# A decoder layer on one core: the fused stage's source rewritten with links a step apart and parts in three places of a step

## The chip, the cores and the metric

The kernel runs on one core of a Trainium2 chip. A core has five engines, each with its own queue of instructions that it works through in order: TensorE (PE, matrix products), VectorE (DVE), ScalarE (ACT), GpSimd (POOL) and SyncE (SP, which here only issues DMAs). Queues meet in semaphores: an instruction that waits holds up all that is behind it in its queue. The metric is the device time of one execution in microseconds (us).

## What is computed

The reference is one decoder layer on `x` of 8 x 512 tokens of 512 features, all in 32-bit floats. Cut to what matters:

```python
x = layernorm(x + mamba(x))          # layernorm, in-projection, convolution over 4 tokens, silu,
                                     # h[t] = exp(A*dt[t]) * h[t-1] + dt[t]*B[t]*x[t]  (1024 channels x 16 states),
                                     # y[t] = sum over states of h[t]*C[t]; y*silu(z), out-projection
x = layernorm(x + attention(x, ctx)) # 16 heads of 32, 512 queries against 512 keys of ctx
x = layernorm(x + moe(x))            # 32 experts, the best 4 of the best 4 groups, 640 places each, and one shared expert
```

Each line needs the one before it, but for one batch row only; the experts need all rows.

## The kernel before

Three stages follow one another: `layers` (mamba, attention, gate and shared expert), `experts`, and `finish` (the last layernorm). The change touches only `layers`, the fused stage, and the helper `layernorm`.

**Chunks and steps.** `layers` runs over 16 chunks: 8 batch rows, each in two halves `t` of 256 tokens. A chunk has 32 steps `k`. A step treats 128 channels and four of the 16 states: four quarters `q` of two channel groups each, four state groups `g`, and the two channel groups in turn. In each step `carry` (L452) allocates one of four buffers `h` and copies the state in, on ACT; `decays` (L446) computes the four exponentials of the *next* step; `scan` forms the input (L458) and runs the recurrence (L462) on DVE; `collect` multiplies by C (L479, DVE) and sums over states with eight matmuls (L483, PE) into the PSUM tile `py`. When a quarter's eight steps are done, `gated` (L495) multiplies the gate `zs` by `py`. The matmuls of a step are the last to read its `h`, so the step four later can only begin when they are done.

**Front work of the mamba part.** Between `scan` and `collect` of certain steps the source calls other functions: `back` of the previous chunk (out-projection, L512, steps 1 and 2), then its residual and layernorm `norm` (L521); `gate_x` (steps 3 to 6), which projects the gate; the silu of `zs` (step 7); `prepare` at steps 3, 11, 19 and 27, which computes `dt` and `dtx` of the next quarter (matmul L398, exponentials L408 to L414 on ACT, `both` L418 to L421 on DVE, and eight DMAs L427 that spread them over partitions); and, for the next chunk, `load_x` (5), `norm_x` (9), `flip_x` (11), `convolve` (12, 15, 18, 21), silu (23) and `x_proj` (24). PSUM for all of these, and for the dense products below, is the tag `mm`, with two buffers.

**Side work.** `sources` and `units` return lists of parts of the attention, the gate and the shared expert of the *previous* batch row: keys and values, queries, the score maxima (`maximum`: L775 on PE, then L777 on DVE), the weights (`weigh`: L801, L805), their sums (`gather`: L817), `divide`, `output`, the gate (`pick`, `choose`, `place`, `locate`), the scatter of tokens to the experts (`send`: L650, indirect DMAs of POOL) and the shared expert (`hidden`, `shared`). Every part has a weight. A running sum of weights, set against `work(k)`, the weight of the mamba part of each step, says how many of them are called in a step, so that the sum grows evenly over two chunks.

**Links.** A part may return a function, its continuation: what DVE or ACT does once PE's product is there. `do` calls a part, then `settle` calls every continuation in `left` once; a continuation may return another, called at the following `settle`. `dry` calls until none is left, and is called where a part is marked `first`.

**Order of the queues.** Before and after, the framework's scheduler decides the order of each engine's queue. It takes the source's order as a preference, but passes over an instruction whose inputs or buffers it takes to be not ready. Only the silu calls and the table load behind them (L362, L363) are tied to the ACT instruction traced before.

Of the kernel before, what the change touches and what calls it, by code (L numbers as in the profile page):

```python
# [17 lines left out]
P = 128  # L18
# [9 lines left out]
T = 256  # L28
# [23 lines left out]
def rsqrt(nc, pool, var, n, name):  # L52

    v = pool.tile([P, n], F32, tag=f"{name}v")
    nc.vector.tensor_scalar(v, var, EPS, None, ALU.add)
    r = pool.tile([P, n], F32, tag=f"{name}r")
    nc.scalar.activation(r, v, AF.Ln)
    nc.scalar.activation(r, r, AF.Exp, scale=-0.5)
    m = pool.tile([P, n], F32, tag=f"{name}m")
    nc.vector.tensor_tensor(m, v, r, ALU.mult)  # L60
    nc.vector.tensor_tensor(m, m, r, ALU.mult)
    nc.vector.tensor_scalar(m, m, -0.5, 1.5, ALU.mult, ALU.add)
    o = pool.tile([P, n], F32, tag=f"{name}o")
    nc.vector.tensor_tensor(o, r, m, ALU.mult)
    return o


def layernorm(nc, pool, tiles, outs, name):

    n = len(tiles)  # L70
    mv = pool.tile([P, n, 2], F32, tag=f"{name}mv")
    for j, t in enumerate(tiles):
        st = pool.tile([P, 6], F32, tag=f"{name}st")
        nc.vector.bn_stats(st, t)
        nc.vector.bn_aggr(mv[:, j, :], st)
    r = rsqrt(nc, pool, mv[:, :, 1], n, name)
    less = pool.tile([P, n], F32, tag=f"{name}less")
    nc.vector.scalar_tensor_tensor(less, mv[:, :, 0], -1.0, r, ALU.mult, ALU.mult)
    for j, (t, o) in enumerate(zip(tiles, outs)):
        nc.scalar.activation(o, t, AF.Identity, bias=less[:, j : j + 1], scale=r[:, j : j + 1])  # L80


def layers(ctx, tc, a, x1d, filld, based, xbuf):
# [193 lines left out]

    def load_x(b, t, f):
        f["xt"] = xt = mp.tile([P, NT_, D], F32, tag="xt", name="xt")
        nc.sync.dma_start(xt, a["x"][b, t * T : (t + 1) * T, :].rearrange("(j p) d -> p j d", p=P))  # L280

    def norm_x(f):
        xt = f["xt"]
        xs = [xt[:, j, :] for j in range(NT_)]
        layernorm(nc, sm, xs, xs, "ln1")
# [34 lines left out]
    def convolve(t, q, f):  # L320
# [4 lines left out]
        def first_tap():  # L325
# [23 lines left out]
            return other_taps  # L349
# [43 lines left out]
    def prepare(q, f):  # L393
# [8 lines left out]
        def exponentials():  # L402
# [13 lines left out]
            def both():  # L416
# [12 lines left out]
                return lambda: timesD  # L429
# [8 lines left out]
            return both  # L438
# [16 lines left out]
    def scan(t, c, g, dtx, bc, da, h):  # L455
# [4 lines left out]
        )  # L460
        flat = h.rearrange("p n t -> p (n t)")
# [4 lines left out]
    def collect(c, g, h, bc, py, f):  # L466


        if g == 0:
            for j in range(2):  # L470
                nc.tensor.matmul(
                    py[j * HP : (j + 1) * HP, c % 2, :],
                    ident[:, j * HP : (j + 1) * HP],
                    f["xs"][c // 2][:, c % 2, :],
                    start=(c % 2 == 0),
                    stop=False,
                )
        steps = h.rearrange("p (j m) t -> p j m t", j=2)[:, :, :, 1:]
        nc.vector.tensor_tensor(steps, steps, bc[1], ALU.mult)  # L479
        for m in range(NG // 2):  # L480
            for j in range(2):
                s = (g, m, c % 2)
                nc.tensor.matmul(  # L483
                    py[j * HP : (j + 1) * HP, c % 2, :],
                    twice,
                    h[:, j * 2 + m, 1:],
                    start=False,
                    stop=(s == (NST // NG - 1, NG // 2 - 1, 1)),
                )

    def gated(q, f, py):

        f["xs"].pop(q)
        pair = f["zs"][:, 2 * q : 2 * q + 2, :]
        nc.vector.tensor_tensor(pair, pair, py, ALU.mult)  # L495
# [6 lines left out]
    def back(half, b, t, f):  # L502
# [15 lines left out]
        def norm():  # L518
# [3 lines left out]
            layernorm(nc, sm, outs, outs, "ln2")  # L522
            r0 = b * S + t * T
            nc.sync.dma_start(x1d[r0 : r0 + T, :].rearrange("(j p) d -> p j d", p=P), o)

        return norm
# [15 lines left out]
    def pick(b, x2t, x2T, st):  # L542
# [8 lines left out]
        return lambda: choose(b, x2t, pl, st)  # L551

    def choose(b, x2t, pl, st):
# [34 lines left out]
        for k in range(K):  # L588
            nc.vector.tensor_reduce(w[:, :, k : k + 1], work, AX.X, ALU.max)
            oh = gm.tile([P, SC, E], F32, tag=f"g_oh{k}", name="g_oh")  # L590
            nc.vector.tensor_tensor(
                oh, work, wide(w[:, :, k : k + 1], [E]), ALU.is_equal
            )
# [3 lines left out]
            nc.vector.tensor_tensor(oh, early, wide(m2, [E]), ALU.is_equal)  # L597
            if k < K - 1:
                nc.vector.scalar_tensor_tensor(work, oh, -4.0, work, ALU.mult, ALU.add)
            picked.append(oh)  # L600
        ws = new([1], "g_ws")
        nc.vector.tensor_reduce(ws, w, AX.X, ALU.add)
        nc.vector.tensor_scalar(ws, ws, 1e-9, None, ALU.add)
        nc.vector.reciprocal(ws, ws)

        any_ = new([E], "g_any")
        nc.vector.tensor_tensor(any_, picked[0], picked[1], ALU.add)
        nc.vector.tensor_tensor(any_, any_, picked[2], ALU.add)
        nc.vector.tensor_tensor(any_, any_, picked[3], ALU.add)
        nc.vector.tensor_tensor(sc, sc, any_, ALU.mult)  # L610
        nc.vector.tensor_tensor(x2t[:, :, D : D + E], sc, wide(ws, [E]), ALU.mult)
        nc.gpsimd.iota(
            x2t.bitcast(I32)[:, :, D + E :], pattern=[[P, SC], [0, 1]], base=b * S, channel_multiplier=1
        )
        st["picked"] = picked, any_

    def place(picked, any_, st):
# [7 lines left out]
        return lambda: locate(picked, pb, pn, st)  # L625

    def locate(picked, pb, pn, st):
# [16 lines left out]
        nc.vector.tensor_scalar(dest, ds_, float(SLOTS), None, ALU.add)  # L644

# [69 lines left out]
    def units(b):  # L715
# [20 lines left out]
        def flip(j):  # L736
            xr = st.pop(("xr", j))
            if j + 1 < SC:
                fetch(j + 1)
# [102 lines left out]
        def divide(oc):  # L842

            attT, total = st["attT"], st["total"]
            r = p3.tile([P, D], F32, tag="row", name="r")
            nc.scalar.activation(r, total, AF.Ln)
            nc.scalar.activation(r, r, AF.Exp, scale=-1.0)
            nc.vector.tensor_tensor(total, total, r, ALU.mult)
            nc.vector.scalar_tensor_tensor(total, total, -2.0, r, ALU.add, ALU.mult)
            nc.vector.scalar_tensor_tensor(  # L850
                attT[:, oc, :], attT[:, oc, :], -1.0, total, ALU.mult, ALU.mult
            )

        def output(lt):
# [9 lines left out]
            def add_up():  # L864
                nc.vector.tensor_tensor(xr, pp, xr, ALU.add)
                nc.vector.tensor_tensor(st["x2"][lt], xr, bo, ALU.add)
                if lt == SC - 1:
                    layernorm(nc, sm, st["x2"], st["x2"], "ln3")
# [12 lines left out]
        def hidden(name, ic):  # L881
# [8 lines left out]
            def use():  # L890
                if name == "sw3":
                    nc.vector.tensor_tensor(hT[:, ic, :], hT[:, ic, :], ps, ALU.mult)  # L892
                    return
                nc.scalar.copy(hT[:, ic, :], ps)
                if ic == DC - 1:
                    silu(hT)
# [20 lines left out]
        todo += more[:-2]  # L917
        add(0, begin)
        add(0, fetch, 0)
        todo += more[-2:]  # L920
        for j in range(SC):
            add(0.5, flip, j)
# [32 lines left out]
        for lt in range(SC):  # L955
            add(3.4, output, lt)
# [11 lines left out]
        for ic in range(DC):  # L968
            add(3.4, hidden, "sw3", ic)
            if ic == (0 if end else 3):  # L970
                add(0.5, lambda: place(*st["picked"], st))
# [3 lines left out]
        for j in range(SC):  # L975
            add(3.4, shared, j, dry=(j == 0))
            if b < B - 1:
                add(*sends[j])
# [24 lines left out]
    left = []  # L1003

    def settle():

        got = [part() for part in left]
        left[:] = [x for x in got if x]

    def dry():  # L1010
        while left:
            settle()

    def do(fn, *args, first=False):

        if first:
            dry()
        rest = fn(*args)
        settle()
        if rest:  # L1020
            left.append(rest)

    def work(k):

        front = 6.9 if k in (1, 2) else 3.4 if 3 <= k < 7 or k in (12, 15, 18, 21, 24) else 1.0 if k in (11, 26) else 0.0
# [3 lines left out]
    norm_x(f)  # L1029
# [14 lines left out]
    decays(0, 0, f["ready", 0][0], das[0])  # L1044
    old, side, cleared = None, [], 0

    for i, (b, t) in enumerate(chunks):
# [7 lines left out]
        py = None  # L1055
        for k, (q, g, ci) in enumerate(steps):
# [5 lines left out]
            h = carry(t, 2 * q + ci, g)  # L1062
# [417 lines left out]
```

## Time and profile before

| | us |
|---|---|
| Median of three runs (5550.69 to 5557.85) | 5556.39 |
| The profiled execution | 5555.79 |
| Its span, from the first to the last instruction | 5554.1 |
| PE busy | 4883.9 (88%) |
| DVE busy | 4349.2 (78%) |
| ACT busy | 2592.8 (47%) |
| POOL busy | 560.9 (10%) |
| First scan to end of the last scan (the fused stage) | 3630.0 |
| From there to the end | 1867.5 |

In the profile, L12 is line 12 of the kernel before. Lines of instructions give start, duration, engine, line, operation, output and inputs with their shapes, a count where several were merged, and in brackets the idle time of the engine just before, with what ended it. Waits are given as who waited, for whom, the total, how often and the longest. Matmuls overlap one another, so PE's busy time says only that it had work. An engine's idle time matters only where that engine is the late one.

### The profile page before, as it was taken

The numbers are of one execution on the slowest core, as the hardware profiler recorded it, in microseconds if no ns is written. First come the engines' busy times: TensorE is split into PE (matmuls) and PEld (weight loads), VectorE is DVE, ScalarE is ACT, GpSimd is POOL, SyncE is SP. The second block draws the span as 40 slices with busy tenths as digits, with TensorE's granted clock in tenths as the row PEclk, the third lists the DMA queues.
The fourth block names the chain that finished last, engine by engine and source line by source line (L and its number), as shares of the span: only waits on it lengthen the run. The fifth ranks groups of instructions, "written<-read, shape, count | busy, mean of one in ns | idle before, by whom it ended". The sixth has DMA issues, their size and how long they took to land. (4 is left out here: it accounts for less than half of the span.)

```text
span 5554.1 us, 60352 instructions
## 1 busy us (share of the span) xinstructions
PE 4883.9 (88%) x19752; PEld 2720.5 (49%) x19752; DVE 4349.2 (78%) x5738; ACT 2592.8 (47%) x5483; POOL 560.9 (10%) x424
## 2 busy tenths in 40 slices
PE   6768889888988988888888898879899999999994
PEld 3334344334434434443443343333577777777773
DVE  7998989989889989899989999864466565555554
ACT  5554565655556555555555655523222222222223
POOL 1000002002000200200010020010111111111111
PEclk7878999999999999999999999989999999999997
DMA  6887345445534634544463464441345444454444
GB/s 183 246 239 203 108 130 184 114 120 154 167 104 113 203 92 129 184 123 113 124 199 104 114 193 110 113 157 44 102 121 125 125 125 124 121 126 124 115 121 146
DMA packets 554282, 769.83 MB, mean 139 GB/s; under 512 B 135754, under 2 KB 268394, under 8 KB 551920
## 3 DMA queue, kind: packets, MB, share of 16 engines
q1 hardware_dynamic: 517952, 677.55, 41.5%
q0 software_dynamic: 33280, 76.90, 7.3%
q10 hardware_dynamic: 2736, 11.54, 0.5%
q8 instruction: 156, 2.56, 0.2%
q14 instruction: 158, 1.29, 0.1%
HBM read 508.68 MB, written 165.05 MB: 121 GB/s over the span
## 5 line engine op out<-in xcount | busy, mean ns | idle before, releaser
L446 ACT ACTIVATE l_da<-both,l_aneg 128x256 f32<-128x256 f32 x2048 | 888.7, 499 | 791.5 <-DVE h L462 744.2
L462 DVE TENSOR_TENSOR_SCAN h<-l_da,h 128x1028 f32<-128x1028 f32 x512 | 1169.4, 2291 | 49.9 <-ACT h L452 27.3
L483 PE MATMUL py<-h,l_twice 128*64 128x256 f32 x4096 | 632.0, 424 | 194.2 <-DVE h L479 194.0
L458 DVE TENSOR_TENSOR h<-both,bc 128x1024 f32<-128x1024 f32 x512 | 617.5, 1213 | 141.8 <-PE py L483 78.2
L479 DVE TENSOR_TENSOR h<-h,bc 128x1024 f32<-128x1024 f32 x512 | 621.9, 1218 | 6.3 <-DMA l_qa<-l_ka 0.3
L483 PEld LDWEIGHTS py<-h,l_twice 128*64 128x64 f32 x4096 | 295.2, 148 | 570.5 <-issue 246.4
L775 PE MATMUL ps_s<-l_ka,l_qa 64*128 64x512 f32 x1024 | 315.2, 695 | 141.9 <-DVE mx L777 141.4
L1230 PE MATMUL ps_h<-xT,w 128*128 128x320 f32 x1536 | 435.6, 433 | 0.0
L1310 POOL DMA_INDIRECT based<-y,xe x160 | 251.2, 1570 | 1313.4 <-ACT y L1333 573.4
L1251 DVE TENSOR_TENSOR hT<-ps_h,p 128x320 f32<-128x320 f32 x128 | 62.9, 491 | 379.1 <-PE ps_h L1230 379.1
L777 DVE TENSOR_REDUCE mx<-ps_s 128x2 f32<-128x1024 f32 x256 | 310.2, 1215 | 56.2 <-PE ps_s L775 55.5
L1230 PEld LDWEIGHTS ps_h<-xT,w 128*128 128x128 f32 x1536 | 292.2, 190 | 118.2 <-issue 0.4
L801 PE MATMUL ps_t<-l_qa,l_ka 64*128 64x512 f32 x1024 | 300.6, 651 | 15.0 <-ACT eT L805 11.4
L805 ACT ACTIVATE eT<-ps_t 128x1024 f32<-128x1024 f32 x256 | 258.7, 1012 | 109.2 <-PE ps_t L801 108.7
L817 PE MATMUL po<-eT,l_va 128*64 128x512 f32 x1024 | 281.5, 628 | 24.6 <-ACT raw L829 20.8
L650 POOL DMA_INDIRECT xbuf<-x2t,dest x128 | 218.7, 1708 | 815.8 <-DVE dest L644 777.4
L1230 PE MATMUL ps_h<-t,s 128*128 128x320 f32 x1024 | 286.1, 432 | 0.0
L712 PE MATMUL ps_p<-x2T,wa 128*128 128x512 f32 x512 | 247.5, 633 | 11.8 <-DVE hT L892 10.3
L311 PE MATMUL ps_z<-xnT,wm 128*128 128x256 f32 x1024 | 241.0, 389 | 17.8 <-DVE o L521 17.0
L311 PE MATMUL ps_x<-xnT,wm 128*128 128x256 f32 x1024 | 242.5, 390 | 2.9 <-DMA wm<-in_in_proj_w 2.0
L512 PE MATMUL po<-wm,zs 128*128 128x512 f32 x512 | 234.6, 608 | 3.9 <-DMA wm<-in_out_proj_w 1.8
L1230 PEld LDWEIGHTS ps_h<-t,s 128*128 128x128 f32 x1024 | 194.6, 190 | 81.1
(234 smaller groups left out, 7414.6 us busy)
## 6 DMA issues: line engine op xcount, KB each, us to landing
bc<-scr SPq DMA_DIRECT2D x1024, 128.0 KB
w<-in_w SPq DMA_DIRECT2D x93, 1024.0 KB
wm<-in_in_proj_w SPq DMA_DIRECT2D x128, 512.0 KB
xbuf<-zero SPq DMA_DIRECT2D x32, 1362.5 KB
xe<-xbuf SPq DMA_DIRECT2D x32, 1362.5 KB
both<-dt SPq DMA_DIRECT2D x256, 128.0 KB
both<-dtx SPq DMA_DIRECT2D x256, 128.0 KB
wm<-in_out_proj_w SPq DMA_DIRECT2D x64, 512.0 KB
```

The source lines that it names most:

```text
L311: nc.tensor.matmul(ps[:, i, :], w[:, dc, i * P : (i + 1) * P], f["xnT"][:, dc, :], start=(dc == 0), stop=(dc == DC - 1),)
L446: nc.scalar.activation(da[:, n, 1:], dt[:, c % 2, j, :], AF.Exp, scale=aneg[:, c, j, g, m : m + 1])
L458: nc.vector.tensor_tensor(steps, dtx[:, c % 2].unsqueeze(2).to_broadcast([P, 2, NG // 2, T]), bc[0], ALU.mult)
L462: nc.vector.tensor_tensor_scan(flat, da.rearrange("p n t -> p (n t)"), flat, 0.0, ALU.mult, ALU.add)
L479: nc.vector.tensor_tensor(steps, steps, bc[1], ALU.mult)
L483: nc.tensor.matmul(py[j * HP : (j + 1) * HP, c % 2, :], twice, h[:, j * 2 + m, 1:], start=False, stop=(s == (NST // NG - 1, NG // 2 - 1, 1)),)
L775: nc.tensor.matmul(ps[:, j, :], qa[r, lt * P : (lt + 1) * P], ka[r, :], start=True, stop=True)
L777: return lambda: nc.vector.tensor_reduce(mx[:, lt, :].unsqueeze(2), ps, AX.X, ALU.max) and None
L801: nc.tensor.matmul(ps[:, j, :], ka[r, kc * P : (kc + 1) * P], qa[r, :], start=True, stop=True)
L805: nc.scalar.activation(eT, ps, AF.Exp)
L817: nc.tensor.matmul(po[j * 2 * HD : (j + 1) * 2 * HD, :], va[:, kc, i, j * HD : (j + 2) * HD], eT[:, j, :], start=(kc == 0), stop=(kc == SC ...
L1230: nc.tensor.matmul(ps, w[:, n, r * P : (r + 1) * P], x[:, n, :], start=not more and n == 0, stop=n == 1, skip_group_check=more,)
```

## The change

- `wait(part)` returns a continuation with a due time: three ticks of a clock that ticks three times a step. `settle` calls only what is due. Most links after the first are wrapped so: `layernorm` comes in three links (statistics, roots, scaling), `norm` a step after `back`, `both` and `timesD` a step each, `other_taps`, the gate's four rounds, `weights`, `place` and `locate`, and the divisions.
- A step's parts are spread over three places: behind `steps_in` (L458's work, now a function of its own) and before the scan, behind the scan and the next step's `carry` and `decays`, and behind the multiply by C.
- The matmuls of `collect` become `products`, called in the following step, before that step's multiply. `py` is allocated there. `gated` moves from step 0 to step 1 of the following quarter.
- The front work moves by about a step: `back` to 2 and 3, `gate_x` to 4 to 7, the silu of `zs` to 8, `load_x` to 7, `norm_x` to 10, `flip_x` to 13, `convolve` to 14, 16, 19, 22, silu to 24, `x_proj` to 25. `prepare` stays at 3, 11, 19 and 27. Side work begins at step 4, and in the second half also at 0 and 1.
- Two rows of `x1` are fetched ahead and not one, the transposes of `x1` go between the last keys of the next batch row, the silu of the shared expert waits for the first place of a step, and the scatters of a batch row are called together in `locate`.

The diff, cut to its core:

```diff
-def layernorm(nc, pool, tiles, outs, name):
+def layernorm(nc, pool, tiles, outs, name, wait=lambda part: part, then=None):
...
+    def roots():
+        r = pool.tile([P, n], F32, tag=f"{name}r")
+        nc.scalar.activation(r, v, AF.Ln)
+        nc.scalar.activation(r, r, AF.Exp, scale=-0.5)
+        def scaled():
...
+        return wait(scaled)
+    return wait(roots)
...
+    left, clock = [], []
+    def wait(part):
+        return (clock[0] + 3 if clock else 0), part
+    def behind(part):
+        return (clock[0] + 3 - (clock[0] + 2) % 3 if clock else 0), part
+    def settle(force=False):
+        due, later = [], []
+        for x in left:
+            (due if force or not clock or x[0] <= clock[0] else later).append(x)
+        for _, part in due:
+            rest = part()
+            if rest:
+                later.append(rest if isinstance(rest, tuple) else (0, rest))
+        left[:] = later
+        return due
+    def dry(force=True):
+        while settle(force):
+            pass
...
-            return other_taps
+            return wait(other_taps)
...
-                return lambda: timesD
+                return wait(timesD)
...
-            return both
+            return wait(both)
...
-    def scan(t, c, g, dtx, bc, da, h):
+    def steps_in(c, h, dtx, bc):
         steps = h.rearrange("p (j m) t -> p j m t", j=2)[:, :, :, 1:]
         nc.vector.tensor_tensor(
             steps, dtx[:, c % 2].unsqueeze(2).to_broadcast([P, 2, NG // 2, T]), bc[0], ALU.mult
         )
+    def scan(t, c, g, da, h):
...
-        return norm
+        return wait(norm)
...
-        return lambda: choose(b, x2t, pl, st)
+        return wait(lambda: choose(b, x2t, pl, st))
...
-        return lambda: locate(picked, pb, pn, st)
+        return wait(lambda: locate(picked, pb, pn, st))
...
+        if clock:
+            for j in range(SC):
+                send(j, st)
...
-            if j + 1 < SC:
-                fetch(j + 1)
+            if j + 2 < SC:
+                fetch(j + 2)
...
-                    silu(hT)
+                    st["silu"] = behind(lambda: st.pop("silu") and silu(hT))
+                    return st["silu"]
...
+            h = ahead
+            parts = []
+            def part(fn, *args, first=False):
+                parts.append((do, fn, *args, first))
...
+            thirds = [[], [], []]
+            for m, x in enumerate(parts):
+                thirds[round((m + 0.5) * 3 / len(parts) - 0.5) if x[0] is do else 1].append(x)
+            def run(m):
+                clock[0] += 1
+                settle()
+                for x in thirds[m]:
+                    if x[0] is do:
+                        do(*x[1:-1], first=x[-1])
+                    else:
+                        x[0](*x[1:])
+            steps_in(2 * q + ci, h, f["ready", q][1], bc)
+            if k % 8 == 1:
+                if k > 1:
+                    gated(q - 1, f)
...
+            run(0)
+            scan(t, 2 * q + ci, g, das[n % 2], h)
+            n += 1
+            if k + 1 < len(steps) or after:
+                nq, ng, ni = steps[(k + 1) % len(steps)]
+                ahead = carry(t if k + 1 < len(steps) else after[1], 2 * nq + ni, ng)
+                decays(2 * nq + ni, ng, (f if k + 1 < len(steps) else nf)["ready", nq][0], das[n % 2])
+            run(1)
+            if products:
+                products()
+            products = collect(2 * q + ci, g, h, bc, f)
+            run(2)
```

## The prediction

> **What bounds the kernel now.** I began with the first part of the page, the busy time of each engine.
>
> ```profile
> PE 4883.9 (88%) x19752; PEld 2720.5 (49%) x19752; DVE 4349.2 (78%) x5738; ACT 2592.8 (47%) x5483; POOL 560.9 (10%) x424
> ```
>
> No engine is full over the span, so I looked at its 40 slices: up to slice 27 both TensorE (PE) and VectorE (DVE) stand at 8 to 9 tenths, after that PE alone. The first of these is the fused stage, which the change rewrites. I cut the span at the first scan and at the end of the last one, and asked for busy times.
>
> ```profile
> core 0: us, PE busy (x) PEld busy (x) DVE busy (x) ACT busy (x) POOL busy (x), PEclk, DMA share, GB/s
> 56.60:3686.60 3630.00, 3088.20 (x12639) 1470.96 (x12638) 3300.43 (x3771) 2047.23 (x4364) 267.09 (x191) 0.92 0.51 148
> 3686.60:5554.10 1867.50, 1757.03 (x6984) 1223.12 (x6983) 1027.89 (x1919) 518.19 (x1064) 283.06 (x195) 0.97 0.46 121
> ```
>
> The fused stage takes 3630.0 us for 512 steps, 7.09 us a step. DVE is busy 3300.4 us and idle 329.6; PE is busy 3088.2 and idle 541.8. No vector instruction of weight is added or removed, so the stage can only change by DVE's idle time: 329.6 us is all that could be won. Who ends that idle time is in the view of waits, for DVE and then for PE, over the fused stage (columns: total us, times, longest):
>
> ```profile
> DVE h L458 <- PE py L483: 78.2, 33, 5.2
> DVE h L458 <- DMA both<-dtx: 43.8, 20, 6.9
> DVE xs L345 <- ACT xs L337: 29.7, 21, 2.8
> DVE h L462 <- ACT h L452: 27.3, 15, 2.0
> DVE zs L495 <- PE py L483: 23.9, 17, 2.4
> DVE st L74 <- DMA xt<-in_x: 12.5, 8, 4.0
> ...
> PE py L483 <- DVE h L479: 194.0, 58, 9.1
> PE ps_s L775 <- DVE mx L777: 140.9, 80, 4.4
> ```
>
> Three kinds stand out. First, DVE waits for PE to free one of the four `h` buffers: 78.2 directly, 27.3 through the copy at L452 on ScalarE (ACT) that itself waits for PE, and 23.9 for the end of a quarter's sum, 129.4 us in 65 waits. Second, 43.8 us for `dtx` of the next quarter. Third, short waits for links of side chains. PE in turn waits 194.0 us for the products' input, L479. So the two queues hold each other up, now one, now the other.
>
> The timeline of DVE, early in one chunk, shows the second kind and how far the queue is from the source:
>
> ```profile
> 1625.36 0.75 DVE L521 SCALAR_TENSOR_TENSOR o<-po,l_rs,o 128x512 f32<-128x512 f32 x1 [0.45 <-PE po L512]
> ...
> 1637.11 2.30 DVE L462 TENSOR_TENSOR_SCAN h<-l_da,h 128x1028 f32<-128x1028 f32 x1 [1.78 <-ACT h L452]
> 1639.33 0.67 DVE L418 SCALAR_TENSOR_TENSOR dtx<-dtx,u 128x512 f32<-128x512 f32 x1
> ...
> 1642.49 0.69 DVE L421 TENSOR_TENSOR dtx<-dt,xs 128x512 f32<-128x512 f32 x1
> ...
> 1650.40 1.23 DVE L458 TENSOR_TENSOR h<-both,bc 128x1024 f32<-128x1024 f32 x1 [2.91 <-DMA both<-dtx]
> ```
>
> L521 belongs to step 3 of the source and stands behind scan 5; L418 belongs to step 4 and stands behind scan 7. DVE's scans run two to three steps ahead of PE's work, as far as four `h` buffers let them, and then the last link of `dtx` is late for step 8.
>
> **What the skill says.** The Trainium skill, "Perfetto Trace Analysis", section "Optimization Strategy", says that where the most contended engine changes over time, interleaving the regimes may help; the mutual waits above agree that it changes. The same page, "Identifying Performance Opportunities", says that a gap repeating on the engine that should be saturated can mean too few buffers for the next tile: the 65 waits on the `h` ring agree. "DMA: Bandwidth & Descriptors", section "Latency and other measured facts", puts a DMA's fixed cost at about 2 us; here the last issue of `dtx` ended at 1648.51 and step 8 began at 1650.40, 1.9 us, which agrees.
>
> **The change part by part.** I price it against the profiled execution: 5555.8 us, span 5554.1, so 1.7 us lies around the span; the median of the runs is 5556.4, the same within 0.6.
>
> *The quarter's `dtx`.* `prepare(1)` moves from behind `gate_x(0)` to before it. That projection is 16 matmuls on PE, 3.72 us in the timeline; the layernorm's two L80 activations (1.52 us), which lie between the exponentials now, move two steps later. Against that `back` is a step later, and `both` comes a step later in source, about where it runs today. At step 8 some 2.5 to 4 us per chunk come off, and the wait there is 2.4 to 4.3 us in most chunks. The other quarters' waits are about 1 us, less than the step by which the products now hold DVE back. I take three quarters of 43.8: **-33 us** (bounds 0 and -44).
>
> *Links a step apart.* Waits of DVE for a link are L345 29.7, L74 12.5, L60 7.6, L418 5.7, L848 3.9, L865 6.1, L521 3.2, L892 2.3 and the gate's first reduction 2.2: 73.2 us, mean about 1 us, longest 5.7, all under the 7.09 us of a step. In source order all would vanish. But the scheduler places a link when it thinks its input ready, so part of the step is taken back: half, **-37 us** (bounds 0 and -73).
>
> *Products a step later.* The eight matmuls L483 of a step are traced behind the first two thirds of the next step's parts. PE then has two thirds of a step, 4.7 us, more before it needs L479; the 58 waits average 3.3 us. But PE's idle time is worth something only where PE is the late one afterwards: one fifth of 194.0, **-39 us** (bounds 0 and -97). I count the spread of `maximum` over three places and the second `fetch` in flight (PE waits 22.6 us for `xr`) in this.
>
> *The price of that.* An `h` buffer comes free two thirds of a step later in PE's order, so DVE may lead by 2.33 steps and not 3. Behind L458 on DVE wait L462, L479 and every L777 that PE's scores need; behind L452 on ACT wait the exponentials. If each of the 65 waits grew by the whole 4.7 us it would cost 306 us; none need grow where DVE's lead is not used up. One sixth: **+51 us** (bounds 0 and 306).
>
> *At nothing.* `norm`, `choose` and `locate` leave their PSUM tiles, two of two for `norm`, a step longer: 29 places, at most 7.09 us each (206 us) if DVE came to them in source order; it reaches L521 two steps beyond its source place, and so finds it due. The input's load goes from step 5 to 7 past SP's broadcasts and its norm from 9 to 10; cover is the three steps between, 21 us; without it L74's 12.5 us grows. The gate's four rounds move over seven steps, and its 16 scatters are issued together: 16 x 1.708 = 27.3 us on POOL, idle 93% of this stage, and next wanted there for the convolution at step 14; `x1T`, which reuses the scattered rows' buffer, comes only after most of the next keys and values. The silu stays a step-wise block: table loads are 61 + 40 at 1283 ns, 130 us of ACT, which is busy 56% here; some loads more or less hide. The tail, in source order without steps, has the same work; its links wait at most one call: 0, within 5 us.
>
> The sum is -33 - 37 - 39 + 51 = -58; 5555.8 - 58 = 5498, I say **5500 us**. Changes within 0.2%, 11 us, can't be told from none.
>
> **Rivals.** (a) *The ring decides: slower.* With four `h` buffers and later products, DVE stalls on L458 and L452 more often than PE is helped. If half the bound comes, 153 us, with the first two gains, 70, and none for PE, the time is 5639. It ends slower once the added ring waits exceed the 109 us of gains, 1.7 us per wait of today. For it: L458 starts within some 2 us of the products' end in long stretches, so the ring is already tight. Against: in other stretches PE follows L479 at once and the ring is slack. (b) *The scheduler undoes it: no change,* 5555. For it: L521 and L418 already run 2 to 3 steps off their source. Against: the order of priority does change on PE, the engine that is behind. (c) *A larger gain:* all link and `dtx` waits go, 117, PE gains a third, 65, ring +51: -131, 5425.
>
> **Chances.** Forecast 0.38 (5460 to 5545), (c) 0.14, (b) 0.10, (a) 0.38. Faster is the first and the third: 0.52. As both signs hold much, the range reaches from (c) to (a), 5410 to 5640; the tail beyond (a), with PSUM held longer, is left out.
>
> **What would show it.** In the changed kernel's waits of the fused stage: L458 for `dtx` below 15 us; the links' waits halved; PE's products for their multiply below 100; the ring's three waits at about 180. DVE busy stays at 3300 and the part after the stage at 1867. Ring waits above 240 make (a) true. A DVE idle sum as now with other names makes (b) true. I am wrong too if links put off by a step reach the next chunk's first step late: that would be waits of L458 for `dtx` or `bc` at step 0, or of L495 for the silu of `zs`.

## The result, and the profile after

The changed kernel takes **5532.44 us** (median of six runs, 5528.46 to 5542.54) against 5557.12 of the kernel before (six runs): ratio **0.9961 [0.9948, 0.9974]**, 24.7 us faster. The sign of the forecast holds; its size, 56 us, is more than twice what came. The time lies within the 5460 to 5545 that the prediction gave its forecast, but, as the waits below show, not by the forecast's terms. The profiled execution of the changed kernel took 5541.2 us, span 5539.5, which is 8.8 us above its median, so the two profiles differ by 14.6 us only.

In the changed kernel L489 is `steps_in` (L458 before), L496 the scan (L462), L503 the multiply by C (L479), L523 the products (L483), L483 the copy of `carry` (L452), L537 `gated` (L495), L449 to L452 `both`, L376 the convolution's taps, L831 and L833 `maximum`, L768 a dense product.

First the busy times over the whole span, from the first part of the changed kernel's page, then the same cut as before: the fused stage, from the first scan to some 3.5 us behind the end of the last one, and the rest (columns as before: length, busy time of PE, PEld, DVE, ACT, POOL with instructions, granted clock, share of DMA, GB/s).

```profile
PE 4900.6 (88%) x19752; PEld 2733.6 (49%) x19752; DVE 4333.6 (78%) x5738; ACT 2544.5 (46%) x5440; POOL 537.8 (10%) x424
```

```profile
56.60:3657.50 3600.90, 3098.37 (x12634) 1482.06 (x12632) 3281.77 (x3764) 1998.11 (x4321) 243.31 (x191) 0.92 0.52 148
3657.50:5539.50 1882.00, 1766.07 (x6992) 1226.34 (x6992) 1030.96 (x1926) 518.92 (x1064) 283.72 (x195) 0.96 0.46 121
```

The fused stage is 29.1 us shorter (3630.0 to 3600.9), the rest 14.5 us longer. In the stage DVE is **busy for 18.7 us less** (3300.43 to 3281.77) and idle for 10.5 us less (329.6 to 319.1). The same 5738 vector instructions are in both kernels, seven of them now in the rest, which is busy 3.1 us more; but the durations of those in the stage sum to only 1.3 us less (3519.0 and 3517.8), so most of the 18.7 us is not less work. Next the view of waits over the fused stage of the changed kernel:

```profile
PE py L523 <- DVE h L503: 176.5, 57, 9.5
PE ps_s L831 <- DVE mx L833: 147.3, 85, 4.4
...
DVE h L489 <- PE py L523: 65.6, 47, 3.4
DVE h L489 <- DMA both<-dtx: 47.0, 14, 6.3
DVE dtx L449 <- ACT dtx L445: 31.4, 16, 6.0
DVE k L753 <- PE ps_p L768: 22.2, 12, 5.2
DVE zs L537 <- PE py L523: 20.3, 13, 4.2
DVE xs L376 <- ACT xs L368: 19.9, 18, 2.2
```

Every wait has a new size, but DVE's named waits add up to 286.8 us where they were 291.5. The ring of `h` buffers fell from 129.4 to 89.9 us (65.6, 4.0 through the copy on ACT, 20.3 at `gated`). The wait for `dtx` did not move (43.8 to 47.0). Of the links, `xs` fell by 9.8 and the input's statistics by 10.1, but the first link of `both` (L449) went from 5.7 to 31.4, and L753, for the keys of the next batch row, is new with 22.2.

So the stage's 29.1 us are 18.7 of busy time, 4.7 of named waits and 5.7 of gaps too short to be named. The busy time is mostly a matter of neighbours. Two pieces of DVE's timeline show it; first the changed kernel:

```profile
1854.68 0.69 DVE L449 SCALAR_TENSOR_TENSOR dtx<-dtx,u 128x512 f32<-128x512 f32 x1
1855.29 0.15 DVE L71 TENSOR_TENSOR m<-v,r 128x2 f32<-128x2 f32 x1
1855.40 0.69 DVE L450 TENSOR_TENSOR l<-l,dtx 128x512 f32<-128x512 f32 x1
1856.01 0.16 DVE L72 TENSOR_TENSOR m<-m,r 128x2 f32<-128x2 f32 x1
1856.13 0.69 DVE L451 TENSOR_TENSOR dt<-dt,l 128x512 f32<-128x512 f32 x1
```

Then the kernel before, where the same small chain (L60 to L62 there) runs back to back:

```profile
1633.26 0.15 DVE L60 TENSOR_TENSOR m<-v,r 128x2 f32<-128x2 f32 x1
1633.44 0.16 DVE L61 TENSOR_TENSOR m<-m,r 128x2 f32<-128x2 f32 x1
1633.64 0.17 DVE L62 TENSOR_SCALAR m<-m 128x2 f32<-128x2 f32 x1
```

Where an instruction needs its neighbour's output, it starts after that one's end: 1633.26 + 0.15 is 1633.41, and the next starts at 1633.44. Where it doesn't, it starts before: L449 ends at 1855.37 and L71 starts at 1855.29, 0.08 us earlier. Alternating the two chains lets each cover the other's latency. Counted over all neighbours on DVE in the whole span, 3662 pairs overlapped before, by 291.5 us in all, and 3846 do now, by 309.4 (in the stage alone 2720 by 218.1 and 2909 by 235.6, 17.5 us more); pairs that follow within 0.1 us of each other fell from 1035 (35.1 us) to 811 (27.9 us). The sum of the durations over the span is the same within 2.2 us (4640.8 and 4643.0).

The split of the stage's 29.1 us into 18.7, 4.7 and 5.7 is made on DVE's side alone. On PE's side the same 29.1 us are 39.3 us less idle time (541.8 to 502.5) and 10.2 us more busy time. So the split says where DVE's time went; that the closer packing caused the gain is not shown by it, and no run below changes the packing alone.

The rest's 14.5 us lie ahead of the first expert's product, which starts 282.0 us after the end of the last scan and not 268.4; from there to the experts' last product of that kind it is 1517 us in both. Work that was left over runs there: the last chunk's out-projection ends 46.3 us after that scan and not 34.2.

### The profile page after: what moved, and what is told of

Read it like the earlier page. It is cut to its first block, busy times and chain, and to the rows that moved or that the text cites. A ratio compares the mean times of both kernels' runs of the same rounds, so it can differ in the third digit from the quotient of the medians.

```text
span 5539.5 us, 60340 instructions
## 1 busy us (share of the span) xinstructions
PE 4900.6 (88%) x19752; PEld 2733.6 (49%) x19752; DVE 4333.6 (78%) x5738; ACT 2544.5 (46%) x5440; POOL 537.8 (10%) x424
## 5 line engine op out<-in xcount | busy, mean ns | idle before, releaser
L496 DVE TENSOR_TENSOR_SCAN h<-l_da,h 128x1028 f32<-128x1028 f32 x512 | 1169.9, 2291 | 18.7 <-ACT h L483 4.0
L523 PE MATMUL py<-h,l_twice 128*64 128x256 f32 x4096 | 636.1, 417 | 176.5 <-DVE h L503 176.5
L489 DVE TENSOR_TENSOR h<-both,bc 128x1024 f32<-128x1024 f32 x512 | 618.9, 1215 | 136.3 <-PE py L523 65.6
L503 DVE TENSOR_TENSOR h<-h,bc 128x1024 f32<-128x1024 f32 x512 | 620.7, 1217 | 5.4
L523 PEld LDWEIGHTS py<-h,l_twice 128*64 128x64 f32 x4096 | 300.5, 146 | 506.9 <-DVE h L503 214.6
L831 PE MATMUL ps_s<-l_ka,l_qa 64*128 64x512 f32 x1024 | 335.2, 698 | 149.1 <-DVE mx L833 148.0
L833 DVE TENSOR_REDUCE mx<-ps_s 128x2 f32<-128x1024 f32 x256 | 310.1, 1215 | 59.3 <-PE ps_s L831 57.9
L768 PE MATMUL ps_p<-x2T,wa 128*128 128x512 f32 x512 | 256.9, 651 | 1.4 <-DVE hT L960 1.4
L831 PEld LDWEIGHTS ps_s<-l_ka,l_qa 64*128 64x128 f32 x1024 | 90.4, 198 | 301.5 <-DVE mx L833 235.8
```

Source lines behind the costliest of these rows:

```text
L489: nc.vector.tensor_tensor(steps, dtx[:, c % 2].unsqueeze(2).to_broadcast([P, 2, NG // 2, T]), bc[0], ALU.mult)
L496: nc.vector.tensor_tensor_scan(flat, da.rearrange("p n t -> p (n t)"), flat, 0.0, ALU.mult, ALU.add)
L523: nc.tensor.matmul(py[j * HP : (j + 1) * HP, c % 2, :], twice, h[:, j * 2 + m, 1:], start=False, stop=(s == (NST // NG - 1, NG // 2 - 1, 1)),)
L831: nc.tensor.matmul(ps[:, j, :], qa[r, lt * P : (lt + 1) * P], ka[r, :], start=True, stop=True)
L833: return lambda: nc.vector.tensor_reduce(mx[:, lt, :].unsqueeze(2), ps, AX.X, ALU.max) and None
```

## The experiments

Four theories stood at the start. *Packing*: the gain is the order that the scheduler makes of a finer source. *Lead*: products a step later give the two engines slack against each other. *Spacing*: links a step apart take DVE's waits away. *Undone*: the scheduler overrules the source, and would do better if tied to it. Ratios are to the kernel before as it was timed with each group of runs (medians of 5550 to 5557 us), with 95% intervals; the changed kernel stands at 0.9961. In "stage" the fused stage is counted to the end of the last scan: 3626.3 us before, 3597.5 after; DVE busy in it 3297.6 and 3279.1, idle 328.6 and 318.3; overlapping pairs are those of the whole span, as above.

### Links at once

```diff
-        return (clock[0] + 3 if clock else 0), part
+        return 0, part
```

> The changed kernel, but a link is due at the next settle again, not a step later; the three places and the later products stay. Theory P (packing: links a step apart put independent work between dependent small VectorE instructions, so that more neighbours overlap): most of the 0.39% is lost, ratio to before 0.998 to 1.002; VectorE's overlap falls from 309 us back towards 292, and instructions that follow within 100 ns of their predecessor's end rise from 811 towards 1035. Theory Q (products a step later give PE and VectorE slack): the gain stays, ratio 0.994 to 0.998. Theory S (any other source order moves the time by some tenths of a per cent, in either direction, through the scheduler's choices): ratio anywhere in 0.990 to 1.010, and no relation to the overlap.

Measured: 5761.8 us, 1.0366 [1.0347, 1.0386]. DVE's busy time stayed at 3275.7 and its pairs at 3829, so packing does not need the spacing; its idle time rose to 531.8. The loss lies in the second chunk of six batch rows (272 to 281 us in place of 236 to 238), in the last step: from its scan to the next chunk's first scan it is 48 to 52 us and not 7.7. PE's timeline there:

```profile
1383.41 1.98 PE L523 MATMUL py<-h,l_twice 128*64 128x256 f32 x8 [3.48 <-DVE h L503]
1388.47 1.98 PE L523 MATMUL py<-h,l_twice 128*64 128x256 f32 x8 [3.08 <-DVE h L503]
1392.50 0.77 PE L676 MATMUL ps_b<-g_any,l_before 128*128 128x128 f32 x2 [2.06 <-DVE g_any L655]
...
1405.54 3.67 PE L399 MATMUL ps_d<-xs,l_w_x 128*64 128x256 f32 x16
...
1412.76 1.12 PE L429 MATMUL ps_dt<-xd,l_w_dt 32*128 32x256 f32 x4
```

And DVE's, some 40 us after the chunk's last scan (1384.80):

```profile
1424.09 0.69 DVE L449 SCALAR_TENSOR_TENSOR dtx<-dtx,u 128x512 f32<-128x512 f32 x1 [8.36 <-ACT dtx L445]
```

PE stands idle twice for DVE's multiply and then for `g_any`, which the gate's `place` (L676) reads; DVE is going through the gate's rounds at that time. Directly behind it the shared expert's 24 products (L768) follow in one block of 12.1 us, which could have filled these gaps. The larger part of the step is what stands behind that block: the next chunk's `x_proj` (L399) and `prepare` (L429). In these six chunks `x_proj` starts 20.0 to 21.6 us after the last scan, where in the changed kernel it starts 28.9 to 29.6 us before it. So DVE has no `dtx` for the next chunk's first step and is mostly idle; that step begins at 1434.05. Over the stage PE waits 307.8 us for L503 (176.5 in the changed kernel). L676 is traced at once, ahead of those products, with one of the two `mm` buffers that `x_proj` and `prepare` use as well. That suggested that one link makes most of the loss.

### Only the gate's links at once, and all but the gate's

The continuations of the gate (`choose`, the rounds, `weights`, `place`, `locate`) are due at once and all others a step later, and the reverse:

```diff
+    def soon(part):
+        return 0, part
...
-        return wait(lambda: choose(b, x2t, pl, st))
+        return soon(lambda: choose(b, x2t, pl, st))
...
-                return wait(best)
-            return wait(weights)
+                return soon(best)
+            return soon(weights)
...
-            return wait(lambda: place(picked, any_, st))
+            return soon(lambda: place(picked, any_, st))
...
-        return wait(lambda: locate(picked, pb, pn, st))
+        return soon(lambda: locate(picked, pb, pn, st))
```

> The reverse: only the gate's links at once, all others a step apart. If the gate alone is the cause, the ratio is 1.025 to 1.040 and VectorE's idle time in the fused stage about 500 us, in the last step of each odd chunk. If it is shared by all links, 1.005 to 1.020.

> The changed kernel with links at the next settle, except the gate's (choose, its rounds, weights, place, locate), which stay a step apart. If the 3.7% of the kernel with all links at once comes from the gate alone (its place, a PE instruction with a PSUM buffer, is traced before its input can be there, and the shared expert's 48 products queue behind it), the ratio is 0.994 to 1.002. If the spacing of the other links is worth what my prediction gave it (37 us), 1.003 to 1.008.

Measured: the gate's alone at once 5697.51 us, 1.0261 [1.0247, 1.0275]; all but the gate's at once 5568.66 us, 1.0033 [1.0022, 1.0044]. So of the 4.1% between the first experiment and the changed kernel 3.0% are the gate's links alone, and the others' spacing is worth 0.7%, some 40 us (0.0072 of 5550). The wait view of PE with the gate's links at once (line numbers are four higher there) has the signature of the first experiment, and `x_proj` of the next chunk is late in the same way (16.9 to 18.4 us after the last scan, and 42.5 to 43.7 us from that scan to the next; with all but the gate's at once it starts 31 to 33 us before it):

```profile
PE py L527 <- DVE h L507: 291.6, 95, 9.5
```

Spacing matters, then, but mostly because here a PE instruction whose input was many vector instructions away was traced ahead of PE's other work, and the next chunk's front work came late behind it. Which of the gate's links does the harm was not tried one by one, nor whether it is the buffer that `place` holds or its place in the queue.

### Other spacings

Two or four ticks in place of three, that is two thirds or four thirds of a step:

```diff
-        return (clock[0] + 3 if clock else 0), part
+        return (clock[0] + 2 if clock else 0), part
```

> The changed kernel with links two thirds of a step apart, and not a step. If the spacing acts smoothly, the time lies between the changed kernel (0.996) and that with links at once (1.037), nearer the first: 0.997 to 1.012, and VectorE's idle time in the fused stage between 318 and 532 us. Theory S: anything in 0.990 to 1.010, not between on purpose.

> The changed kernel with links four thirds of a step apart. If more spacing gives more slack, the ratio is 0.990 to 0.996. If the step was the right distance, chains reach the quarter's start late, VectorE's waits for dtx rise above 80 us, and the ratio is 1.000 to 1.010.

Measured: two ticks 5597.65 us, 1.0086 [1.0072, 1.0099]; four ticks 5537.46 us, 0.9971 [0.9961, 0.9982]. With 0, 2, 3 and 4 ticks DVE is idle 532, 371, 318 and 319 us. Of these spacings one step is enough: four thirds add nothing, and at two thirds the kernel is slower than before the change, most of it again in the last step of those six chunks (23.8 to 27.1 us between the two scans).

### Products in their own step

`products` is called in its own step behind the multiply, and `gated` stands at step 0 again:

```diff
...
-            if products:
-                products()
...
             products = collect(2 * q + ci, g, h, bc, f)
+            products()
```

> The changed kernel with one part undone: the eight products of a step are traced in their own step, behind its multiply by C, and gated goes back to step 0 of the next quarter (before the multiply). Theory P: the gain stays, ratio 0.994 to 0.998. Theory Q: it goes, ratio 0.999 to 1.004, VectorE's waits on the h ring rise from 90 us to about 130, and PE's waits for the multiply (176 us) rise to about 195. My prediction's step on the ring said the reverse for the ring: waits there fall below 90. Theory S: anything in 0.990 to 1.010.

Measured: 5581.32 us, 1.0047 [1.0033, 1.0060]: this part, taken out, costs 0.9%. DVE's busy time fell further, to 3269.9, with 3956 pairs, but it was idle 371.0. The ring's wait at L489 was 79.2 (65.6 in the changed kernel), so with earlier products it is no smaller; the wait for `dtx` was 119.0 in 23 waits (47.0 in 14). With its products in their own step DVE runs into the quarter's `dtx`, which at step 8 of the chunks alone costs 77.2 us (30.3 in the changed kernel).

### Products a step later, alone

The kernel before, with only `collect` cut in two, `products` called in the next step and `gated` moved to step 1:

```diff
-            collect(2 * q + ci, g, h, bc, py, f)
+            if later:
+                later()
+            later = collect(2 * q + ci, g, h, bc, f)
...
-            if k % 8 == 0:
-                if k:
-                    gated(q - 1, f, py)
+            if k % 8 == 1:
+                if k > 1:
+                    gated(q - 1, f)
```

> The kernel before with one part of the change alone: the eight products of a step are traced in the following step, before its multiply; gated goes to step 1 of the next quarter. My prediction's terms give -39 + 51, so 5569 us (ratio 1.002, between 0.997 and 1.009). If the parts work only together (each of them taken from the changed kernel cost 0.9% to 4%), the ratio is above 1.003. If scatter of the scheduler's choices explains all (theory S), anything in 0.990 to 1.010 is as likely.

Measured: 5552.91 us, 0.9995 [0.9987, 1.0003]: nothing. The window and the waits of DVE over its fused stage say why:

```profile
56.50:3698.70 3642.20, 3094.21 (x12641) 1477.27 (x12640) 3325.99 (x3792) 2031.19 (x4357) 220.49 (x195) 0.92 0.51 147
```

```profile
DVE h L458 <- PE py L488: 63.6, 51, 4.5
DVE h L462 <- ACT h L452: 35.2, 15, 2.6
DVE o L526 <- PE po L517: 33.9, 15, 6.2
```

The wait for `dtx` is down to 1.4 us and the ring's waits fell to 111.2 (63.6, 35.2 and 12.4 at `gated`; 129.4 before). DVE's idle time fell by 14.3. But it is busy 3324.3 us to the end of the last scan, 26.7 more than before: some 16 are longer durations in sum (21 of its instructions came into the stage from the rest, which is 8.8 us shorter), some 11 are neighbours that overlap less (3476 pairs for 3662). And PE's wait for the multiply, which the later products were to shorten, is 213.1 us and not 194.0. What DVE won in waits is lost again in busy time.

### Three places, alone

The kernel before with its parts spread over three places of the step, links as they were (called at each `settle`):

```diff
-            scan(t, 2 * q + ci, g, f["ready", q][1], bc, das[n % 2], h)
-            n += 1
+            steps_in(2 * q + ci, g, f["ready", q][1], bc, h)
...
+            thirds = [[], [], []]
+            for m, x in enumerate(parts):
+                thirds[round((m + 0.5) * 3 / len(parts) - 0.5) if x[0] is not finish else 1].append(x)
```

> The kernel before with another part alone: the parts of a step are called in three places, front work at the same steps as before, links at the next settle, products in their own step. If the three places give the closer packing on VectorE (busy 3279 us in the fused stage with them, 3298 and 3301 without), VectorE is busy about 3280 us here too, overlaps rise from 3662 towards 3850, and the ratio is 0.993 to 0.998 if nothing else changes. If the places need links a step apart, VectorE's idle time rises by 50 us or more and the ratio is above 1.003.

Measured: 5597.32 us, 1.0083 [1.0070, 1.0096]; pairs 3653, busy time 3298.6, idle 369.7. Alone the three places pack nothing, and the waits for `dtx` (70.6), `py` at `gated` (60.4) and the taps (55.5) grow.

### One place

The changed kernel with all of a step's parts behind the scan:

```diff
-                thirds[round((m + 0.5) * 3 / len(parts) - 0.5) if x[0] is do else 1].append(x)
+                thirds[1].append(x)
```

> The changed kernel, but all parts of a step are called in one place, behind the scan. Theory P: VectorE's parts stand less mixed with the step's own instructions, ratio 0.997 to 1.001. Theory Q: no change from the changed kernel, 0.994 to 0.998, and PE's 147 us of waits for the maxima stay within 15. Theory S: anything in 0.990 to 1.010.

Measured: 5594.92 us, 1.0074 [1.0060, 1.0087]. The packing goes back to what it was before the change (3670 pairs, busy 3300.8), and the ring's wait at L489 doubles to about 130 us. DVE's idle time rises to 377.6. So in the changed source the three places carry the packing, and a good part of the waits too; the two were not separated.

### Queues tied to the source

The queues of PE, DVE and ACT, then of PE alone, are held to the order of the source inside the steps:

```diff
+            got = fn(*args, **kw)
+            if self.on:
+                self.tc.keep_in_program_order(got)
+            return got
...
+    nc = Tied(tc, ('vector', 'tensor', 'scalar'), clock)
```

> The changed kernel with the queues of PE, VectorE and ScalarE tied to the source's order within the fused stage's steps; the work is the same. If the scheduler is what takes the gain of the new source order back (my rival b), the waits for links (86 us on VectorE, and 22 for the keys' products) and for the next quarter's dtx (47) nearly vanish and the time falls by 60 to 150 us, ratio 0.973 to 0.989. If the four h buffers are the limit, VectorE's ring waits grow beyond 200 us and the ratio is above 1.0.

> The changed kernel with PE's queue alone tied to the source's order. With PE, VectorE and ScalarE tied it took 2.5% longer than before, of which VectorE's busy time (3413 us against 3279) is the larger part. If the packing on VectorE is the cost of tying, it stays at 3280 to 3300 here and the ratio is 0.990 to 1.000. If PE in source order loses by itself, VectorE's idle time is above 370 us and the ratio above 1.004.

Measured: three queues tied 5689.05 us, 1.0247 [1.0233, 1.0261]; PE alone 5631.25 us, 1.0148 [1.0134, 1.0162]. With all three tied, 2534 pairs overlap and 2081 follow within 0.1 us. The window over its fused stage, and a piece of its timeline on DVE (every instruction carries the line of the wrapper, L105):

```profile
55.50:3843.90 3788.40, 3124.91 (x12716) 1488.83 (x12717) 3415.46 (x3803) 1961.80 (x4315) 210.72 (x201) 0.90 0.49 142
```

```profile
1810.48 0.15 DVE L105 TENSOR_TENSOR m<-v,r 128x4 f32<-128x4 f32 x1
1810.67 0.16 DVE L105 TENSOR_TENSOR m<-m,r 128x4 f32<-128x4 f32 x1
1810.87 0.17 DVE L105 TENSOR_SCALAR m<-m 128x4 f32<-128x4 f32 x1
1811.07 0.16 DVE L105 TENSOR_TENSOR r<-r,m 128x4 f32<-128x4 f32 x1
```

In source order each link's chain runs without anything between, one start every 0.2 us for 0.16 us of work. DVE is busy 134 us more than in the changed kernel: 32 us are longer durations in sum (39 more instructions are in the stage), and 100 us are overlap that is gone, 0.08 us for each of the 1293 pairs that overlap no more in the stage. With PE alone tied, DVE's pairs fall to 3679 and its idle time is 401.6: the order on PE alone changes both. The scheduler does overrule the source, and that is worth 2.9% here. The theory that it undoes the change falls.

### A fifth buffer in the ring

The changed kernel with five `h` buffers; `bc`, six deep, gives one up for the space:

```diff
-        h = mp.tile([P, NG, T + 1], F32, tag="h", name="h", bufs=4)
+        h = mp.tile([P, NG, T + 1], F32, tag="h", name="h", bufs=5)
```

> The changed kernel with five h buffers and not four; the broadcast tiles pay for it with five buffers and not six. If the ring of h is what holds the two engines together, its 90 us of VectorE's waits fall below 40 and the ratio is 0.984 to 0.992. If VectorE then only runs ahead into the next quarter's missing dtx, those 47 us rise by as much as the ring's fall, and the ratio is 0.994 to 1.000.

Measured: 5546.66 us, 0.9993 [0.9985, 1.0002], slower than the changed kernel by 0.3%. Its profile is that of an execution 15 us above the median. The waits of DVE over its fused stage:

```profile
DVE h L489 <- DMA both<-dtx: 139.4, 27, 8.7
DVE h L489 <- PE py L523: 56.6, 24, 6.8
```

The ring's waits fall and those for `dtx` rise from 47.0 to 139.4. So behind the ring DVE runs into the quarter's first step, where `dtx` is late. Whether the late `dtx` bounds the changed kernel is the next question.

### An earlier `dtx`

`prepare` for the next quarter at steps 1, 9 and 17 of a chunk in place of 3, 11 and 19; in the changed kernel, in the changed kernel with five `h` buffers and five `bc`, and in the kernel before (there ahead of `back`):

```diff
-            if k % 8 == 3:
-                if q + 1 < CC // 2:
-                    part(prepare, q + 1, f)
-                elif after:
-                    part(prepare, 0, nf)
+            if k % 8 == 1 and q + 1 < CC // 2:
+                part(prepare, q + 1, f)
+            if k == 27 and after:
+                part(prepare, 0, nf)
```

> The changed kernel with prepare of the next quarter at steps 1, 9 and 17 and not 3, 11 and 19. If the late dtx is the bound, VectorE's waits for it fall from 47 us to under 10; as the ring is still four deep, part of it comes back there (90 us, to 110): the time falls by 10 to 40 us, ratio 0.988 to 0.994. If the dtx wait is only one of several waits with the same length, the ring takes all of it and the ratio stays at 0.995 to 0.998.

> The same with five h buffers (and five broadcast tiles). If dtx bounds the lead, its 139 us fall below 40 and nothing else takes their place: ratio 0.978 to 0.988. If PE is the real bound, the ring's waits or those for the end of a quarter's sum rise instead, and the ratio is above 0.993.

> The kernel before with prepare at steps 1, 9 and 17, ahead of back. Its waits for dtx, 44 us, go below 10; if they were worth their length, ratio 0.991 to 0.996. If the ring takes them over, 0.997 to 1.003; if prepare ahead of back costs the next chunk's chain a PSUM buffer, above that.

Measured: 5522.79 us, 0.9949 [0.9935, 0.9962] alone; **5491.95 us, 0.9892 [0.9877, 0.9907]** with five buffers; 5587.07 us, 1.0064 [1.0050, 1.0078] in the kernel before. The window and the waits of DVE of the second:

```profile
56.10:3628.40 3572.30, 3063.55 (x12626) 1476.05 (x12625) 3289.77 (x3784) 1994.03 (x4319) 276.02 (x191) 0.93 0.52 150
```

```profile
DVE h L489 <- PE py L523: 67.8, 48, 3.0
DVE zs L537 <- ACT zs L393: 25.8, 7, 4.1
DVE xs L376 <- ACT xs L368: 25.0, 15, 3.3
```

The wait for `dtx` is no longer among the larger ones. By itself the move takes that wait away too, but brings little over the changed kernel (their intervals overlap): DVE is still idle for 316.5 us (318.3), in other waits, 75.0 of it for the ring at L489. So the late `dtx` alone is not the bound. The fifth buffer, which lost by itself, now gains: DVE is idle 282.4 us where the changed kernel had 318.3; pairs (3818) and busy time (3286.3) are close to the changed kernel's. The ring's wait at L489 hardly moves with it (75.0 to 67.8); the idle time falls in many small waits, most in that of `both` for L445 (16.0 to 0.5). How the fifth buffer brings this about is not shown. This is the best version of the study: 60 us under the kernel before and some 40 under the changed one. In the kernel before the same move also takes the wait for `dtx` away, and loses: the scan waits 62.3 us for the copy of `carry` on ACT there, which the change calls half a step earlier (4.0 in the changed kernel), and DVE is busy for 15.9 us more, with 3517 pairs. Five buffers in the kernel before were not tried, nor the shift of the front work by a step on its own.

## Why the prediction was right or wrong

**"The stage can only change by DVE's idle time": wrong.** No vector instruction of weight was added, as it said, but busy time depends on who stands beside whom. Of the stage's 29.1 us 18.7 are busy time (at most 1.3 of them work that left the stage), a further 5.7 short gaps, and only 4.7 DVE's named waits, on which three of the four terms stood. "DVE busy stays at 3300" failed: 3281.77.

**The quarter's `dtx`, -33: measured +3.** At step 8, where 2.5 to 4 us a chunk were to come off, the waits sum to 30.3 us before and after; at step 16 they grew from 6.7 to 16.9. The step counted what left PE ahead of `prepare(1)` and not where DVE would be by then: DVE leads the source as far as the ring lets it. With five buffers it runs further ahead, and the wait is 139.4. In the changed kernel it goes where `prepare` itself moves, by two steps (the last experiments); in the kernel before it also goes with the late products alone (1.4).

**Links a step apart, -37: measured about +13 on the same waits (73.2 to 85.8), and 22.2 for L753 besides.** Each link was expected to gain by itself. But with the new places and spacing other links are late (L449, L753). Within the changed source the spacing is worth much: some 40 us for all but the gate's, and 3.0% for the gate's, a price that the prediction had put "at nothing".

**Products a step later, -39: the waits went from 194.0 to 176.5, not below 100.** Alone the part is worth nothing (0.9995), within the change 0.9% (products in their own step: 1.0047). Some slack between the two queues is there, but it shows in DVE's `dtx` and ring waits; PE's wait for the multiply rose to 213.1 with the part alone.

**The price of the ring, +51: the sign was wrong.** The ring fell by 39.5 to 89.9, and to 111.2 with the late products alone. The buffers do come free later: from the end of a multiply to the end of its products it is 14.5 us on average before and 16.5 after, 2.0 more and not the 4.7 of two thirds of a step. But DVE came to a freed buffer 6.4 us after that on average before, and 4.5 now, so most steps had the 2.0 us to spare. The ring's waits became more and shorter: 65 of 2.0 us, then 75 of 1.2. Why their sum fell is not shown.

**Rivals.** (a), the ring decides: refuted, at 89.9 where it needed 240. (b), the scheduler undoes it: its sign in the waits did come (286.8 named for 291.5, other names), yet the time fell, by a path which none of the rivals had. Tying the queues shows the scheduler as a help. (c) had the same terms as the forecast and fails with them.

**The rest.** "1867 after the stage" came out at 1882.0 in the profile: left-over work ahead of the experts gave back half of the stage's gain. It is 1867.9 with links at four ticks, and 1863.5 in the best version, so it is not a fixed price of the change.

The forecast was thus right in sign by luck: the two gains on DVE (-33 and -37) did not come and the cost (+51) did not either, so that its named waits fell by 4.7 us together, and most of what DVE gained stands in its busy time, a term that the prediction had excluded. Why the three places pack only beside the rest of the change (3846 pairs; alone 3653) is not settled. What differs is that the layernorm and the gate come in separate pieces there, and with those at once, but still in pieces, packing stayed (3829); the cut itself was not tried alone.

## What to carry to other kernels

On an engine with many short instructions look at the starts and ends of neighbours before taking its busy time as fixed: here two independent chains woven together took less of its time than one after the other, and counts of overlapping pairs show it. Less busy time alone is no gain, though: with products in their own step, and with a fifth buffer, DVE was busy for less (3269.9 and 3262.4) and the kernel was slower. When an engine leads its source through a ring of buffers, find what it would wait for next before adding a buffer: here the fifth lost 0.3% until the late input had been moved, and then both together gained 0.7% on the changed kernel. A link that puts an instruction on a busy queue, with a buffer that others need, is better traced when its input is near: here the gate's links traced at once cost 3.0%.

## What the runs showed of the hardware

- An instruction on DVE that does not need its neighbour's output starts 0.08 to 0.09 us before that one's recorded end; one that does mostly starts 0.03 to 0.10 us after it (0.03 from scan to multiply, 0.10 from `steps_in` to scan). The Trainium skill, "Perfetto Trace Analysis", section "Per-engine timelines", says that the recorded time of a DVE instruction runs until its writes are acknowledged, while the next may begin to fetch its data when the execution ends. That agrees with the overlap. Nearly the same vector work (3749 and 3800 instructions in the stage, durations of 3517.8 and 3548.3 us in sum) was recorded as 3262.4 and 3413.0 us busy, with 4010 and 2534 overlapping pairs.
- ACT loaded tables 138 times before and 95 times in the changed kernel, at 1283 ns each, and ACT's busy time in the stage fell by 49 us. With 107 loads, and `prepare` earlier with four `h` buffers, the time was no longer than with 95, which does not speak against the prediction that a few loads more or less are hidden.
